# Layer 0 of a four-layer convolution kernel: columns evaluated at points as well as rows, and the weights of layers 1 and 2 kept in memory

## The chip, the cores and the metric

The kernel runs on one core of a Trainium2 chip. A core has five engines that run their own instruction streams in order: TensorE (PE in the profile) multiplies matrices into PSUM, VectorE (DVE), ScalarE (ACT) and GpSimd (POOL) work on elements, and SyncE (SP) issues most of the transfers. Transfers issued by SP and by ACT run on the same 16 DMA engines. The metric is the device time of one execution, in microseconds. The kernel before took 4069.13 us in the median of three runs (4066.38 to 4071.3).

## The reference, cut to what matters

The input is a batch of four images of 256 channels and 48 by 48 pixels. Four layers follow each other, each added to its input after a group normalisation. Only the first three concern us.

```
# layer 0: a 7x7 convolution, dilation 2, padding 6, 256 -> 128 channels
k = relu(conv(gn(x), w1, dilation=2, padding=6) + b1)
attn = softmax(relu(bn(conv1x1(k, w2) + b2)))          # 49 weights for each pixel
out  = sum over the 49 taps p of  shift(gn(x), p) * attn[p]
x = x + out
# layer 1: 3x3 convolution, sign of gn(x), sign of the weights
x = x + conv(sign(gn(x)), sign(wl1), padding=1)
# layer 2: 3x3 convolution with ternary weights and a scale for each output channel
x = x + conv(gn(x), alpha * ternary(wl2), padding=1)
# layer 3: windowed linear attention, unchanged here
```

## The kernel before, in words

**Layer 0.** A dilation of 2 splits an image into four phases (even and odd rows, even and odd columns), each a plain 24 by 24 image under a 7x7 convolution. The kernel computes the convolution by rows in the manner of Winograd and Toom-Cook: four output rows at a time, `MT = 4`, from seven evaluation points `POINTS = (0.0, None, 0.5, 1.0, -1.0, 2.0, -2.0)`, where `None` stands for infinity. For each point, VectorE combines input rows (`seen_at`, line 471 does the arithmetic), TensorE convolves the combined rows with the combined kernel rows (`conv0`, line 515), and VectorE adds the result, with a scale, into four output rows (lines 529 and 533). The seven kernel rows are handled as two parts (rows 0 to 3, rows 4 to 6), so every point but infinity has two parts. Along columns the convolution is direct: seven taps. One `conv0` call thus makes 2 parts x 2 halves of the image x 2 channel tiles x 7 taps = 56 matrix products of 288 output columns, and 28 at infinity.

**Weights of layer 0.** `transform_weights` (line 289 for arithmetic, line 283 for the stores) computes the combined kernel rows at the five points that are neither 0 nor infinity and stores them in DRAM through the SP queue. `load_wt` (line 256) loads one part for each use into one of three buffers, `wtp`. The points 0 and infinity need no combination: their weights are loaded straight from the input.

**After the convolution.** `activate0` (line 540) makes `k1`. `attention` (lines 555 to 571) makes the 49 weights for a block of five phase rows and stores them as a band matrix in DRAM; its work tile `e` has two buffers. `apply0` (lines 616 to 637) loads the bands, transposes them and multiplies.

**Layers 1 and 2.** `prepare_layer1` and `prepare_layer2` compute the signs and the ternary weights once, with scales, and keep them in SBUF as `wl1_sb` and `wl2_sb`. `conv3x3` (line 650) uses them for every image. Layer 2 runs as two half images.

**Order.** The main loop goes over images. Within image b, the seven `conv0` calls are interleaved with the rest of image b-1: attention after the first, `apply0` after the second and third, layer 1 after the fourth, the two halves of layer 2 after the fifth and sixth. So the convolution of one image fills TensorE while the other image waits for something. For image 0, where there is no image before, `prepare_layer1` and `prepare_layer2` take those places. The row combinations of the next image's points 0 and infinity are made inside the last call but one. A scheduler then reorders instructions by its own estimates of time and fixes an order for each engine and queue; the tile pools add waits for free buffers. Layer 3 (line 126 for all its operations) is written in a fixed order and runs after all of this, from about 1640 us on.

The lines of the main loop that set the interleaving:

```
ahead = {1: (0.5,), 2: (1.0, -1.0), 4: (2.0, -2.0)}
for f, p in enumerate(POINTS):
    conv0(f, vs.pop(p), rows)
    if f in ahead:
        vs.update(seen_at(pads[b], ahead[f]))
    if f < len(rest):
        rest[f]()
```

Of the kernel before, what the change touches and what calls it, by code (L numbers as in the profile page):

```python
# [10 lines left out]
F32 = mybir.dt.float32  # L11
BF16 = mybir.dt.bfloat16
# [7 lines left out]
P = 128  # L20
# [18 lines left out]
MT = 4  # L39
# [5 lines left out]
NTH = NT // 2  # L45
# [84 lines left out]
def conv_preact_kernel(  # L130
# [35 lines left out]

    wt_d = {
        (f, part): dram.tile([C, K0, P], F32, tag=f"wt{f}_{part}", name=f"wt{f}_{part}")
        for f, p in enumerate(POINTS)
        for part in range(2)  # L170
        if p
    }
    x3_d = [dram.tile([C, H, W], F32, tag=f"x3_{b}", name=f"x3_d{b}") for b in range(B)]
# [3 lines left out]
    def rsqrt(r, t, n):  # L177

        s = small.tile([P, n], F32, tag=f"rsq_s{n}", name="rsq_s")
        u = small.tile([P, n], F32, tag=f"rsq_u{n}", name="rsq_u")  # L180
        nc.scalar.activation(s, t, AF.Sqrt)  # L181
        nc.vector.reciprocal(r, s)
        nc.vector.tensor_mul(u, t, r)
        nc.vector.tensor_mul(u, u, r)
        nc.vector.tensor_scalar(u, u, -0.5, 1.5, ALU.mult, ALU.add)
        nc.vector.tensor_mul(r, r, u)
# [37 lines left out]
    with (  # L224
# [3 lines left out]
        tc.tile_pool(name="vp", bufs=3) as vp,  # L228
        tc.tile_pool(name="wtp", bufs=3) as wtp,
        tc.tile_pool(name="op0", bufs=1) as op0,  # L230
        tc.tile_pool(name="ps_cv", bufs=3, space=PSUM) as ps_cv,
# [12 lines left out]
        def rows_at(a):  # L244

            return w1[:, a * K0 : (a + 1) * K0, :].rearrange("(ct p) k o -> p ct k o", p=P)

        def load_wt(f, part):
            wt = wtp.tile([P, NCT, K0, P], F32, tag="wt", name="wt")
            p = POINTS[f]  # L250
            if p:
                src = wt_d[f, part].rearrange("(ct p) k o -> p ct k o", p=P)
            else:
                src = rows_at((MT - 1 if p is None else 0) + MT * part)
            for ct in range(NCT):
                nc.sync.dma_start(out=wt[:, ct], in_=src[:, ct])
            return wt

        def transform_weights():

            at = {p: f for f, p in enumerate(POINTS)}
            n = 0
            with tc.tile_pool(name="wst", bufs=2) as wst:
                for ct in range(NCT):
                    for k0, k1 in ((0, 4), (4, K0)):
# [16 lines left out]
                        def put(p, part, t):  # L282
                            nc.sync.dma_start(
                                out=wt_d[at[p], part][ct * P : (ct + 1) * P, k0:k1, :],
                                in_=t.rearrange("p (k o) -> p k o", o=P),
                            )
# [13 lines left out]
                        for p in (1.0, 2.0):  # L300
                            even, odd = new("we", 2), new("wo", 2)
                            stt(even, g[2], p * p, g[0])
                            stt(odd, g[3], p * p, g[1])
                            for s in (p, -p):
                                t = new("wr", 4)
                                stt(t, odd, s, even)
                                put(s, 0, t)
                            stt(even, g[6], p * p, g[4])
                            for s in (p, -p):
                                t = new("wr", 4)  # L310
                                stt(t, g[5], s, even)
                                put(s, 1, t)
# [36 lines left out]
        wl1_sb = wts.tile([P, NCT, T1, C], BF16, name="wl1_sb")  # L349
        wl2_sb = wts.tile([P, NCT, T1, C], F32R, name="wl2_sb")  # L350
        alpha = wts.tile([P, NCT], F32, name="alpha")

        def prepare_layer1():
            stage = padp.tile([P, NCT, T1, C], F32, tag="pad", name="wl1_stage")
            nc.sync.dma_start(out=stage, in_=wl1.rearrange("(ct p) t o -> p ct t o", p=P))
            nc.scalar.activation(wl1_sb, stage, AF.Sign)

        def prepare_layer2():
# [34 lines left out]
            for i, (ct, g) in enumerate(groups):  # L393
# [7 lines left out]
                nc.vector.tensor_sub(wl2_sb[:, ct, 3 * g : 3 * g + 3], u, v)  # L401
# [98 lines left out]

        def conv0(f, v, rows):

            p = POINTS[f]
            parts = range(1 if p is None else 2)
            pss = [
                ps_cv.tile([P, NPH, NTH, HP], F32, tag="cv", name="cv0") for half in range(2)
            ]
            vt = v.rearrange("p c (f t) w -> p c f t w", t=NTP)
            for part in parts:
                wt = load_wt(f, part)  # L510
                for half in range(2):
                    t0 = NTH * half + part
                    for ct in range(NCT):
                        for k in range(K0):
                            nc.tensor.matmul(  # L515
                                pss[half],
                                wt[:, ct, k, :],
                                vt[:, ct, :, t0 : t0 + NTH, k : k + HP],
                                start=((part, ct, k) == (0, 0, 0)),
                                stop=((part, ct, k) == (parts[-1], NCT - 1, K0 - 1)),  # L520
                            )
            for half in range(2):
                src = pss[half].rearrange("p f t w -> p (f t w)")
                for j in range(MT):
                    if scales[f][j] == 0.0:
                        continue
                    dst = rows[:, half, j, :]
                    if any(scales[i][j] != 0.0 for i in range(f)):
                        nc.vector.scalar_tensor_tensor(  # L529
                            dst, src, scales[f][j], dst, ALU.mult, ALU.add  # L530
                        )
                    else:
                        nc.vector.tensor_scalar_mul(dst, src, scales[f][j])

        def activate0(rows):

            k1 = op0.tile([P, NPH, HP * HP], F32, tag="k1", name="k1")
            for half in range(2):
                for j in range(MT):
                    nc.scalar.activation(  # L540
                        k1.rearrange("p f (h t j w) -> p h j f t w", h=2, t=NTH, j=MT)[:, half, j],
                        rows[:, half, j, :].rearrange("p (f t w) -> p f t w", f=NPH, t=NTH),
                        AF.Relu,
                        bias=b1_sb,
                    )
            return k1
# [92 lines left out]
        def conv3x3(parts, w_sb, evacuate, first, rbs):  # L639


            for mo in range(NCT):
                for rb in rbs:
                    ps = ps_cv.tile([P, RB, W], F32, tag="cv", name="cv3")
                    n = 0
                    for ct in range(NCT):
                        for t in range(T1):
                            r0, c0 = rb * RB + t // 3 - first, t % 3
                            for pad in parts:
                                nc.tensor.matmul(  # L650
                                    ps,
                                    w_sb[:, ct, t, mo * P : (mo + 1) * P],
# [5 lines left out]
                    evacuate(ps, mo, rb)  # L658

        def layer1(xt, b):  # L660
# [15 lines left out]
            conv3x3([pad], wl1_sb, evacuate, 0, range(NRB))  # L676

        def layer2(xt, b):
# [14 lines left out]
            def half_image(half):  # L693
# [12 lines left out]
                for ct in range(NCT):  # L706
# [20 lines left out]
                    wl2_sb,  # L727
# [28 lines left out]
        with (  # L756
# [4 lines left out]
            for b in range(B + 1):  # L761
# [33 lines left out]
                rows = op0.tile([P, 2, MT, NPH * NTH * HP], F32, tag="rows0", name="rows0")  # L795
# [829 lines left out]
```

## Time and profile before

| what | value |
|---|---|
| median of the runs | 4069.13 us |
| profiled execution, its own time | 4058.38 us |
| its span (first to last instruction) | 4056.6 us |
| granted TensorE clock over the span, mean | 0.955 of full speed |
| TensorE busy | 3580.7 us (88%) |
| VectorE busy | 2179.4 us (54%) |
| ScalarE busy | 950.8 us (23%) |
| GpSimd busy | 1446.2 us (36%) |
| start to the end of image 0's convolution | about 257 us |
| one turn of the loop over images (from the first `conv0` of an image to that of the next) | 372 us (632 to 1004 to 1376) |

The page gives busy times over the span, and then the span in 40 equal slices of 101 us. Layers 0 to 2 take slices 1 to 16. The trace can be asked for single stretches: a timeline gives start, duration, engine, line, operation and tiles, the count of merged instructions, and in brackets how long the engine sat idle before and who released it. One matrix product in float32 leaves two records, so that 364 products for each image are 728 records.

### The profile page before, as it was taken

How to read it: one execution, taken by the hardware profiler on the slowest of the kernel's cores; microseconds unless marked ns; L12 is line 12 of the kernel's file. 1: busy time of each engine (PE TensorE's matmuls, PEld its weight loads, DVE VectorE, ACT ScalarE, POOL GpSimd, SP SyncE). 2: the span in 40 equal slices, each digit the busy share in tenths (PEclk: the TensorE clock that was granted, in tenths of full speed). 3: DMA queues.
4: the chain of work that ended last, by engine and by line, in shares of the span. 5: the costliest groups of instructions: out<-in, count | busy, mean ns of one | idle time of the engine just before them, and what ended most of it. 6: DMA issues, size and time to landing. Idle time of an engine off the chain costs nothing. (4 is left out here: it accounts for less than half of the span.)

```text
span 4056.6 us, 70470 instructions
## 1 busy us (share of the span) xinstructions
PE 3580.7 (88%) x27940; PEld 2141.2 (53%) x27940; DVE 2179.4 (54%) x4704; ACT 950.8 (23%) x1863; POOL 1446.2 (36%) x2097
## 2 busy tenths in 40 slices
PE   5999998999899788678888888889998999988898
PEld 4777696778768668333334343344444444444443
DVE  7633325324332222466776666676666766556655
ACT  0101100100010110344422233332334423233321
POOL 0000000010001001244777557765645766444432
PEclk9999999999899778899999999999999999999999
DMA  7334015102510402333345434444422444210211
GB/s 280 129 63 73 28 65 64 56 19 83 71 40 19 39 23 74 100 108 129 126 145 150 116 100 135 139 145 118 130 74 95 134 124 124 68 40 29 60 56 55
DMA packets 364763, 367.85 MB, mean 91 GB/s; under 512 B 187123, under 2 KB 327443, under 8 KB 362003
## 3 DMA queue, kind: packets, MB, share of 16 engines
q1 hardware_dynamic: 358771, 353.84, 31.3%
q10 hardware_dynamic: 5520, 8.00, 0.6%
q8 instruction: 222, 3.64, 0.4%
q0 software_dynamic: 144, 1.52, 0.2%
q14 instruction: 106, 0.87, 0.1%
HBM read 249.47 MB, written 115.30 MB: 90 GB/s over the span
## 5 line engine op out<-in xcount | busy, mean ns | idle before, releaser
L126 DVE TENSOR_TENSOR sm<-s,masks 128x112 f32<-128x112 f32 (+10 forms) x2592 | 1135.5, 493 | 800.6 <-PE s L126 349.5
L126 POOL TENSOR_TENSOR sm<-sm,masks 128x432 f32<-128x432 f32 (+14 forms) x1152 | 853.2, 754 | 984.2 <-ACT sm L126 713.0
L126 PE MATMUL s<-qs,ks 32*128 32x320 f32 (+3 forms) x5760 | 825.9, 502 | 202.4 <-DVE sm L126 143.2
L126 ACT COPY sm<-s 128x528 f32<-128x528 f32 (+2 forms) x1152 | 594.1, 534 | 1512.9 <-PE s L126 1220.9
L126 PE MATMUL acc<-sm,vs 128*32 128x384 f32 (+18 forms) x13440 | 882.4, 386 | 13.8 <-POOL sm L126 13.7
L515 PE MATMUL cv<-v,wt 128*128 128x288 f32 x2912 | 763.2, 417 | 29.1 <-DVE v L471 21.0
L126 PEld LDWEIGHTS s<-qs,ks 32*128 32x128 f32 x5760 | 369.6, 187 | 609.2 <-DVE sm L126 216.6
L515 PEld LDWEIGHTS cv<-v,wt 128*128 128x128 f32 x2912 | 546.9, 191 | 194.6 <-issue 19.2
L126 PEld LDWEIGHTS acc<-sm,vs 128*32 128x32 f32 x13440 | 355.6, 111 | 549.0 <-issue 348.1
L650 PE MATMUL cv<-pad,wl_sb 128*128 128x384 f32 (+1 forms) x2592 | 472.1, 344 | 17.3 <-ACT pad L721 12.1
L650 PEld LDWEIGHTS cv<-pad,wl_sb 128*128 128x128 f32 x1728 | 319.5, 192 | 18.3 <-issue 12.3
L459 POOL MEMSET v<- 128x192 f32 x28 | 8.3, 297 | 786.2 <-issue 421.3
L529 DVE SCALAR_TENSOR_TENSOR rows<-cv,rows 128x288 f32<-128x288 f32 x144 | 57.1, 451 | 284.4 <-PE cv L515 284.4
L126 POOL TENSOR_TENSOR pt<-pt 128x144 f32<-128x144 f32 x336 | 183.4, 546 | 23.1 <-DVE pt L126 1.0
L126 POOL TENSOR_TENSOR nhi<-nhi,nq 128x384 f32<-128x384 f32 x144 | 149.7, 1066 | 0.0
L683 DVE SCALAR_TENSOR_TENSOR x<-cv,alpha,x 128x384 f32<-128x384 f32 x48 | 29.7, 618 | 222.1 <-PE cv L650 222.1
L181 ACT ACTIVATE rsq_s<-gn_v 128x2 f32<-128x2 f32 x16 | 3.3, 203 | 556.7 <-DVE gn_v L208 556.6
L126 PE MATMUL out_ps<-o,wout_sb 128*128 128x384 f32 x288 | 123.2, 510 | 9.9 <-DVE o L126 5.9
L126 PE MATMUL proj_ps<-wv_sb,xn 128*128 128x256 f32 x288 | 87.5, 434 | 42.7 <-ACT vt L126 21.8
L627 PEld LDWEIGHTS ap<-seen,xT 120*128 120x128 f32 (+2 forms) x832 | 115.4, 221 | 13.7 <-ACT seen L620 11.8
L627 PE MATMUL ap<-seen,xT 120*128 120x120 f32 (+3 forms) x832 | 119.4, 306 | 1.9 <-ACT seen L620 1.8
L650 PEld LDWEIGHTS <-wl_sb 128*128 128x128 bf16 x864 | 84.9, 99 | 63.6 <-issue 4.8
(157 smaller groups left out, 2549.1 us busy)
## 6 DMA issues: line engine op xcount, KB each, us to landing
wt<-wt SPq DMA_DIRECT2D x80, 448.0 KB
kb_d<-pt SPq DMA_DIRECT2D x48, 576.0 KB
rc<-r_d SPq DMA_DIRECT2D x192, 144.0 KB
nhi<-kb_d SPq DMA_DIRECT2D x120, 192.0 KB
nlo<-kb_d SPq DMA_DIRECT2D x88, 192.0 KB
o_d<-stage SPq DMA_DIRECT2D x24, 576.0 KB
o<-o_d SPq DMA_DIRECT2D x24, 576.0 KB
xr<-x_d SPq DMA_DIRECT2D x33, 384.0 KB
```

The costliest lines, as they stand in the source:

```text
L126: return lambda *args, **kwargs: self.tc.keep_in_program_order(op(*args, **kwargs))
L181: nc.scalar.activation(s, t, AF.Sqrt)
L459: nc.gpsimd.memset(v[:, :, :, 0:PADP], 0.0)
L515: nc.tensor.matmul(pss[half], wt[:, ct, k, :], vt[:, ct, :, t0 : t0 + NTH, k : k + HP], start=((part, ct, k) == (0, 0, 0)), stop=((part, c ...
L529: nc.vector.scalar_tensor_tensor(dst, src, scales[f][j], dst, ALU.mult, ALU.add)
L627: nc.tensor.matmul(pf[:, f, a:e], xTs[k + i][:n, f, mo * P : (mo + 1) * P], seen[:n, 1 + i, a:e], start=(i == 0), stop=(i == near[-1]),)
L650: nc.tensor.matmul(ps, w_sb[:, ct, t, mo * P : (mo + 1) * P], pad[:, ct, r0 : r0 + RB, c0 : c0 + W], start=(n == 0), stop=(n == len(parts) ...
L683: nc.vector.scalar_tensor_tensor(xs, ps, alpha[:, mo : mo + 1], xs, ALU.mult, ALU.add)
```

## The change

Columns are now treated like rows: two output columns at a time (`MX = 2`), seven taps split as 2+2+3, and four column points (1, -1, 0 and infinity). `columns_at` makes, for each row point, four tensors of column combinations from `v` on VectorE. `conv0` then makes, for each column point, products with three combined taps (one at infinity) over a whole image, so 288 output columns as before, and combines four PSUM results into `y`, which then goes into the rows. The combined weights have four column variants for each row point, also at the row points 0 and infinity. They are made by `put_columns`, with additions on GpSimd and stores on the ACT queue. `load_wt` loads one column point at a time.

To make room, the weights of layers 1 and 2 no longer stay in SBUF: `prepare_layer1` and `prepare_layer2` write them to DRAM, and `load_wl1` and `load_wl2` load them again for every use into the same buffers as layer 0's weights, `wtp`, now four. `vp` goes from three buffers to two, the temporaries `we` and `wo` from two to one.

The core of the diff:

```diff
-        tc.tile_pool(name="vp", bufs=3) as vp,
-        tc.tile_pool(name="wtp", bufs=3) as wtp,
+        tc.tile_pool(name="vp", bufs=2) as vp,
+        tc.tile_pool(name="wtp", bufs=4) as wtp,
+        tc.tile_pool(name="yp", bufs=2) as yp,
...
+        def load_wt(f, g):
+            src = wt_d[f, g]
+            n = src.shape[1] * src.shape[2]
+            wt = new_wt()[:, 0 : NCT * n].rearrange("p (ct a) o -> p ct a o", ct=NCT)
+            nc.sync.dma_start(
+                out=wt, in_=src.rearrange("(ct p) a k o -> p ct (a k) o", p=P)
+            )
...
+        def put_columns(f, part, c0, c1, t, ks, new):
+            def put(g, k0, k1, v):
+                for ct in range(c0, c1):
+                    nc.scalar.dma_start(
+                        out=wt_d[f, g][ct * P : (ct + 1) * P, part, k0:k1, :], in_=v[:, ct - c0]
+                    )
+            n = c1 - c0
+            if ks[0] == 0:
+                pairs = t[:, :, 0:4, :].rearrange("p c (k i) o -> p c k i o", i=2)
+                g0, g1 = pairs[:, :, :, 0, :], pairs[:, :, :, 1, :]
+                for g in (1, -1):
+                    u = new("wu", [P, n, 2, P])
+                    for c in range(n):
+                        (nc.gpsimd.tensor_add if g > 0 else nc.gpsimd.tensor_sub)(
+                            u[:, c], g0[:, c], g1[:, c]
+                        )
+                    put(g, 0, 2, u)
+                put(0, 0, 2, g0)
+            if ks[1] == K0:
+                g0, g1, g2 = (t[:, :, 4 - ks[0] + i, :] for i in range(3))
+                e = new("wx", [P, n, P])
+                nc.gpsimd.tensor_add(e, g0, g2)
+                for g in (1, -1):
+                    u = new("wu", [P, n, P])
+                    (nc.gpsimd.tensor_add if g > 0 else nc.gpsimd.tensor_sub)(u, e, g1)
+                    put(g, 2, 3, u.unsqueeze(2))
+                put(0, 2, 3, g0.unsqueeze(2))
+                put(None, 0, 1, g2.unsqueeze(2))
...
+                for i, (p, part, a) in enumerate(((0.0, 0, 0), (0.0, 1, MT), (None, 0, MT - 1))):
+                    raw = op0.tile([P, NCT, K0, P], F32, tag=("k1", "rows0")[i % 2], name="w1_row")
+                    nc.scalar.dma_start(out=raw, in_=w1[:, a * K0 : (a + 1) * K0, :]...)
+                    put_columns(at[p], part, 0, NCT, raw, (0, K0), new_x)
...
+            for mo in range(NCT):
+                signs = new_wt().bitcast(BF16)...
+                nc.scalar.activation(signs, stage[:, :, :, mo * P : (mo + 1) * P], AF.Sign)
+                nc.sync.dma_start(out=wl1_d[mo], in_=signs)
...
+                ternary = new_wt()[:, 0 : 3 * NCT]
+                nc.vector.tensor_sub(ternary.rearrange("p t m o -> p t (m o)"), u, v)
+                for mo in range(NCT):
+                    nc.sync.dma_start(
+                        out=wl2_d[mo, ct, :, 3 * g : 3 * g + 3, :], in_=ternary[:, :, mo, :]
+                    )
...
+        def columns_at(v):
+            n = NPH * NTP - 1
+            vx = {}
+            for g in XPOINTS:
+                t = vp.tile([P, NCT, NPH * NTP, NXP], F32, tag="vx", name="vx", bufs=8)
+                dst = t[:, :, 0:n, :]
+                i, j = {1: (1, 2), -1: (2, 1), 0: (0, 2), None: (1, 3)}[g]
+                u, w = (v[:, :, 0:n, k : k + MX * (NXP - 1) + 1 : MX] for k in (i, j))
+                (nc.vector.tensor_add if g == 1 else nc.vector.tensor_sub)(dst, u, w)
...
+            for g in XPOINTS:
+                wt = load_wt(f, g)
+                ps = ps_cv.tile([P, NPH, NT, NX], F32, tag="cv", name="cv0")
+                todo = [(part, i, k, ct) for part in parts
+                        for i, k in enumerate(XPARTS[g]) for ct in range(NCT)]
+                for n, (part, i, k, ct) in enumerate(todo):
+                    nc.tensor.matmul(ps, wt[:, ct, part, i, :],
+                                     vx[g][:, ct, :, part : part + NT, k : k + NX], ...)
+                if g == 1:
+                    for j in range(MX):
+                        nc.scalar.mul(y[:, :, j], ps, 0.5)
+                elif g == -1:
+                    for j, sign in enumerate((0.5, -0.5)):
+                        nc.vector.scalar_tensor_tensor(y[:, :, j], ps, sign, y[:, :, j], ...)
+                elif g == 0:
+                    nc.vector.tensor_add(y[:, :, 0], ps, y[:, :, 0])
+                else:
+                    nc.vector.tensor_sub(y[:, :, 1], y[:, :, 1], ps)
...
+        def load_wl2(mo):
+            w_sb = []
+            for ct in range(NCT):
+                wt = new_wt()[:, 0:T1]
+                nc.sync.dma_start(out=wt, in_=wl2_d[mo, ct])
+                w_sb.append(wt.bitcast(F32R))
+            return w_sb
```

## The prediction

> **What bounds the kernel now.** I read the page's slices first, then the costliest groups, then TensorE's timeline through layers 0 to 2, then its waits there.
>
> The slices (40, 101 us each):
>
> ```profile
> PE   5999998999899788678888888889998999988898
> DVE  7633325324332222466776666676666766556655
> ...
> PEclk9999999999899778899999999999999999999999
> ```
>
> Layers 0 to 2 are slices 1 to 16: TensorE is full, VectorE two to three tenths busy. The change touches nothing after them, so layer 3's stretch (1640 to 4057 us) is taken as it is. The group it rests on, and its consumer:
>
> ```profile
> L515 PE MATMUL cv<-v,wt 128*128 128x288 f32 x2912 | 763.2, 417 | 29.1 <-DVE v L471 21.0
> L529 DVE SCALAR_TENSOR_TENSOR rows<-cv,rows 128x288 f32<-128x288 f32 x144 | 57.1, 451 | 284.4 <-PE cv L515 284.4
> ```
>
> The layer-0 products take 763.2 us, with 29.1 us idle before them in all; VectorE waits for them, not they for VectorE. TensorE's timeline (start, duration, count; idle before in brackets):
>
> ```profile
> 36.21 7.59 PE L515 MATMUL cv<-v,wt 128*128 128x288 f32 x24 [8.13 <-DMA wt<-in_w_dram]
> ...
> 90.22 29.68 PE L515 MATMUL cv<-v,wt 128*128 128x288 f32 x112 [9.95 <-DVE v L471]
> 119.74 1.46 PE L380 MATMUL abs_ps<-wl_tmp,ones 128*128 128x256 f32 x6
> ...
> 140.35 0.83 PE L409 MATMUL sum_ps<-ones,wl_tmp 128*128 128x1 f32 x6
> ...
> 305.42 1.81 PE L555 MATMUL lg<-w_sb,k 128*120 128x49 f32 x8 [6.35 <-DVE e L560]
> ...
> 527.32 27.90 PE L515 MATMUL cv<-v,wt 128*128 128x288 f32 x112
> ...
> 632.05 26.18 PE L515 MATMUL cv<-v,wt 128*128 128x288 f32 x98 [3.87 <-DVE v L471]
> ...
> 679.69 1.80 PE L555 MATMUL lg<-w_sb,k 128*120 128x49 f32 x8 [7.04 <-DVE e L560]
> ...
> 697.74 0.63 PE L616 MATMUL tra<-ident,rows 120*120 120x120 f32 x2 [5.73 <-DMA rows<-band_d]
> ```
>
> In image 0 the small products of layer 2's preparation (119.7 to 198 us) sit between convolution products; its convolution ends at 257. From image 1 on a turn takes 372.0 us, 344 to 350 of them TensorE work. What TensorE waits for between 250 and 1660 us (total, times, longest):
>
> ```profile
> PE lg L555 <- DVE e L560: 39.2, 9, 13.5
> PE tra L616 <- DMA rows<-band_d: 26.1, 9, 10.5
> ```
>
> So the loop is TensorE's, with small holes in attention that convolution products fill until they run out.
>
> **What the Trainium skill says.** "TensorE: Matmul & The Clock Gate", Part 1: after about 3.4 us of idling TensorE runs at half clock until about 3.4 us of work. The trace agrees: the logits after 6.35 us of idling took 1.81 us instead of 0.94. "DMA: Bandwidth & Descriptors", Anatomy of one DMA: a transfer has about 2 us of fixed cost, mostly the receipt of the write. Here the load that depends on a weight store ending its issue at 60.7 was issued at 63.25, 2.5 us later. "Trainium Kernel Development and Optimization", Key Constraints: queues of SP, ACT and POOL share 16 DMA engines, and several issuers save only issue time. No row of before shows ACT issuing in such a mass. "GPSIMD Engine Reference", 3.1: an elementwise addition is 1.96 times as slow there as on VectorE; the trace has 1.07 us against 0.56 for 384 elements.
>
> **Part 1: products removed, images 1 to 3.** Before 6 x 56 + 28 = 364 products an image; after, 40 at each of six points (3+3+3+1 taps, two parts, two channel tiles) and 20 at infinity, 260. That is 104 products or 208 records fewer. A warm stretch gives 27.90/112 = 0.249 us a record, the whole group 763.2/2912 = 0.262, cold stretches included. I take the second: 54.5 us an image, **-163.5** for three. All of it is on the bound. Runs of 12 columns in place of 24 I price at nothing, since both make 288 columns a product; bounds 0 and +0.05 us a record (0.30).
>
> **Part 2: image 0, which gains nothing.** Its start becomes weight-bound. All column variants are now made: about 61 GpSimd additions of 256 elements at 0.67 us and 60 of 128 at about 0.5 are 71 us; VectorE, before it reaches layer 2's preparation, has 88 row combinations (0.53), 27 row points (0.845), 16 column combinations (1.05) and small work, 98 us from 46 on, so not before 143. The ACT queue has some 182 weight stores, 7 raw loads and a few activations ahead of layer 1's signs. With three `wu` buffers a result costs 0.67 (add) + 0.45 (issue) + 2.5 (store lands) = 3.7 us for a buffer, 1.2 us each; 80 of them are 98 us from 50 on, and the three raw loads behind each other on the same queue add some 17: **165 us** for the last store, 0.82 us an ACT entry. Below: 143, where VectorE and GpSimd set it. Above: 1.3 us an entry, 244.
>
> Queued behind it: the signs of layer 1 (ACT, 4.0 us), then SP's stores of those signs, behind which stand loads of point 0.5's later column weights. TensorE so resumes about 175. The rest of that point is 14 us (189). Then six groups of absolute sums (2.55 pitch, 15.3: 204), threshold and copies 2.7, and six groups of sums at 9.0 (pitch 9.8 before, less the 0.8 of convolution between), 54: 261. In the changed instruction order all sums stand ahead of the convolution of point 1.0 except its first column pairs, so TensorE mostly idles where it used to convolve. A cold clock adds 8 (269), and four points at 80 records x 0.249 = 19.9 end at **349** against 257: **+92**.
>
> **Part 3: the turns, +50.** A point's convolution is now 20 us, not 28, and two points surround attention. Turn 0 to 1: column combinations and padding of the next image have 4 us of convolution above them instead of 20, +5; attention's next block waits for its band store (about 11 us to land) with 30 us of filler, not 42, +5. Turns 1 to 2 and 2 to 3: in the changed order VectorE's padding and row points of the next image stand behind attention's first `e`, which waits for the logits, for `k1` and so for all of the last `conv0`. From its end: y 0.8, rows 3.6 (four of 576 elements at 0.75 and the normalisation), `k1` 2.8, logits 1.8, `e` 1.2, padding 3.25, row points 13.5, first columns 1.0: 28 us idle, before 1.37 + 3.87. That is +23; attention begins earlier and saves 6 of its 14 us of holes, +17 a turn, **34**. Cold restarts at 3 each: 6. Sum 10 + 34 + 6.
>
> Costed at nothing, with their cover: VectorE's additions, per point four columns x 1.07, four y operations x 0.45, four rows x 0.75 less eight x 0.45, +5.5 us, 36 an image; 132 becomes 168 of about 320. Two ACT multiplications a point (about 0.5). Both lie under 20 us of products; without that cover 5.5 and 1 a point. Weight loads: 2.6 MB a point and 5.9 MB for layers 1 and 2, against a DMA share of 0.22 to 0.26 in the loop; four buffers of at least 5 us each are issued 14 us ahead. If those loads came late, each point would lose what it lacks of 20 us. Layer 2's halves: a chain of 13 us under 20 (under 28 before). After image 3 nothing moves.
>
> **Sum.** 4056.6 + 92 + 50 - 163.5 = 4035 for the span; the median of the runs lies 12.5 above this span (4069.1, the profiled execution 4058.4). **4048**.
>
> **Rivals.**
> *A, the stores are quick and the turns hardly stall.* Last store at 143 (-22), turns +10 (-40): 3986. For it: GpSimd idle until slice 9; against: `e` before the padding in the order.
> *B, slower: the ACT store queue.* One mechanism at the start: every entry of about 190 issues more slowly than 0.82 us, because each waits for its addition on GpSimd, whose buffer waits for an earlier store. It decides from 0.95 us an entry (last store at 186: 21.5 us more, all the margin). At 1.3 us, 244, it gives 4127. For it: stores of 512-byte to 1 KB rows, with SP's loads on the same engines; against: DMA share three tenths there before.
> *C, the turns eat half of the gain* (weights for layers 1, 2 and 0 arrive late through one SP queue): 81 us lost, about 4130. Against: share 0.25.
> *D, the change does not do what it says:* a product over 12-column runs costs more. At 0.30 us a record 0.05 x 2080 = 104: 4150. Against: other shapes in the trace run at their column count.
>
> **How the numbers follow.** Forecast case, 4010 to 4061: 0.40. A: 0.12. Within 0.2% (4061 to 4077), what a measurement of this kernel can just tell from no change: 0.13. B: 0.23. C and D: 0.12. So faster 0.52, same 0.13, slower 0.35. The time is the first case's, 4048; its own range is 4010 to 4061. For 8 in 10, A reaches down to 3995 and B up to 4135; that leaves out half of A, D and the slowest of B.
>
> **What the profile after would show.** 2080 records of layer-0 products at 0.25 to 0.26 us (part 1, D). The last weight store on ACT near 165 and TensorE free from idling near 175 (part 2; 143 is A, beyond 186 B). TensorE mostly idle during the sums, image 0's convolution over near 349. Idle of 26 to 28 us before the first products of images 2 and 3, ended by VectorE's columns (A: below 10). A turn of 372 - 54.5 + 17 + 3 = about 338. Products released by weight loads in the loop would be C. Layer 3 unchanged at 2417. The prediction is wrong if the pace of ACT's entries leaves 0.7 to 0.95, if the scheduler's order leaves TensorE other work during the sums, or if the hole at a turn is not one chain.

## The result

The changed kernel takes 4117.26 us in the median of four runs (4107.39 to 4120.82). The kernel before, run beside it, takes 4070.22 (4066.38 to 4078.06). The ratio is 1.0109, interval 1.0086 to 1.0133: slower by about 1.1%, or 47 us, where 21 us less were forecast. The time lies inside the wide range given (3995 to 4135), outside that of the forecast case (4010 to 4061), and on the other side of no change. The profiled executions have spans of 4118.6 and 4056.6 us, a difference of 62: that of after is the slowest of its four runs (4120.8), that of before (4058.4) quicker than any run listed, so the sums below, made between profiles, are some 15 us too large in all.

Where the 62 us are, with the ends of convolutions taken from TensorE's timelines by counting records:

| stretch, us | before | after | difference | forecast |
|---|---|---|---|---|
| start to the end of image 0's convolution | 256.9 | 386.8 | +129.9 | +92 |
| from there to the end of image 3's convolution | 1113.2 | 1040.2 | -73.0 | -113.5 |
| the rest | 2686.5 | 2691.6 | +5.1 | 0 |

**The slices of after**, 40 of 103 us, in the order of those shown of before:

```profile
PE   3169889699788969578888898889989989988998
DVE  7645532752653222356777657676666775656655
POOL 4500000001000001244678747775646675444332
PEclk9569899799889979799989999999999999999999
```

TensorE is busy three tenths and one tenth in the first two slices, where it was full before, and its clock falls there and in each turn (a turn is one pass of the loop over images). GpSimd, idle at the start before, has the column weights to make.

**The costliest groups of after**: the layer-0 products, and the new column combinations that feed them.

```profile
L612 PE MATMUL cv<-vx,wt 128*128 128x288 f32 x2080 | 557.4, 425 | 119.5 <-DVE vx L592 65.2
L592 DVE TENSOR_TENSOR vx<-v 128x868 f32<-128x868 f32 x112 | 120.8, 1091 | 35.6 <-PE cv L612 35.6
```

The change does what it says: 2080 records for 2912, 205.8 us of work less, or 51.5 an image. But the idle before these products went from 29.1 to 119.5 us, and VectorE now releases much of it.

**TensorE's timeline of after**, through image 0, and at the turn from image 1 to image 2 (start, duration, count, idle before):

```profile
63.88 22.68 PE L612 MATMUL cv<-vx,wt 128*128 128x288 f32 x80 [32.19 <-DVE vx L592]
89.50 10.66 PE L612 MATMUL cv<-vx,wt 128*128 128x288 f32 x36 [2.94 <-issue]
146.58 2.29 PE L612 MATMUL cv<-vx,wt 128*128 128x288 f32 x4 [46.42 <-ACT y L622]
197.46 1.53 PE L698 MATMUL trx<-ident,pad 128*120 128x128 f32 x6 [48.59 <-ACT xT L703]
198.78 21.72 PE L612 MATMUL cv<-vx,wt 128*128 128x288 f32 x80
...
240.95 1.44 PE L490 MATMUL sum_ps<-ones,wl_tmp 128*128 128x1 f32 x6 [6.43 <-DVE wl_tmp L485]
...
252.48 1.44 PE L490 MATMUL sum_ps<-ones,wl_tmp 128*128 128x1 f32 x6 [5.02 <-DVE wl_tmp L485]
...
370.95 15.87 PE L612 MATMUL cv<-vx,wt 128*128 128x288 f32 x64
...
576.92 19.67 PE L612 MATMUL cv<-vx,wt 128*128 128x288 f32 x80
...
753.62 22.56 PE L612 MATMUL cv<-vx,wt 128*128 128x288 f32 x80 [16.49 <-DVE vx L592]
```

Two row points are done by 149 us, with a hole of 46 us in them; then nothing until 197; from 241 to 301 only the small sums of layer 2's preparation, with no convolution between them, each group at 1.44 us instead of 0.72. Once TensorE is warm (at full clock), a point takes 19.67 us for its 80 records.

What ended the two holes is in **ACT's timeline of after**, the queue's issues and its own work in one order:

```profile
146.09 0.43 ACT L622 ACTIVATE y<-cv 128x288 f32<-128x288 f32 x1 [4.59 <-DMA wt<-wr]
...
192.29 0.45 ACTq L276 DMA_DIRECT2D wt_None<-wr  x1
192.79 4.13 ACT L430 ACTIVATE wt<-wl_stage 128x2304 bf16<-128x2304 f32 x2 [46.27 <-DMA wt<-wu]
196.84 1.05 ACT L703 COPY xT<-trx 120x512 f32<-120x512 f32 x2
```

The last weight store is issued at 192.3; layer 1's signs and the copies that TensorE's transposes wait for stand behind it. Why no convolution runs beside the sums is in **SP's timeline of after**:

```profile
284.15 0.89 SPq L480 DMA_DIRECT2D wl_d<-wt  x2
285.14 0.46 SPq L265 DMA_DIRECT2D wt<-wt  x1
```

The first column weights of point 1.0 are loaded (L265) at 285.1, after the fifth of the six stores of ternary weights (L480).

### The profile page after: what moved, and what is told of

It is laid out like the page before. It is cut to its first block, busy times and chain, and to the rows that moved or that the text cites. A ratio compares the mean times of both kernels' runs of the same rounds, so it can differ in the third digit from the quotient of the medians.

```text
span 4118.6 us, 69754 instructions
## 1 busy us (share of the span) xinstructions
PE 3411.3 (83%) x27108; PEld 2021.9 (49%) x27108; DVE 2354.4 (57%) x4840; ACT 968.8 (24%) x1904; POOL 1552.0 (38%) x2218
## 5 line engine op out<-in xcount | busy, mean ns | idle before, releaser
L612 PE MATMUL cv<-vx,wt 128*128 128x288 f32 x2080 | 557.4, 425 | 119.5 <-DVE vx L592 65.2
L612 PEld LDWEIGHTS cv<-vx,wt 128*128 128x128 f32 x2080 | 406.0, 199 | 235.2 <-DVE vx L592 65.9
L759 PE MATMUL cv<-pad,wt 128*128 128x384 f32 (+1 forms) x2592 | 479.0, 348 | 18.7 <-ACT pad L844 6.1
L759 PEld LDWEIGHTS cv<-pad,wt 128*128 128x128 f32 x1728 | 324.5, 195 | 17.5 <-issue 12.5
L806 DVE SCALAR_TENSOR_TENSOR x<-cv,alpha,x 128x384 f32<-128x384 f32 x48 | 29.7, 618 | 220.9 <-PE cv L759 220.9
L592 DVE TENSOR_TENSOR vx<-v 128x868 f32<-128x868 f32 x112 | 120.8, 1091 | 35.6 <-PE cv L612 35.6
L759 PEld LDWEIGHTS <-wt 128*128 128x128 bf16 x864 | 85.9, 100 | 66.8 <-issue 10.2
L133 PE MATMUL out_ps<-stage,wout_sb 128*128 128x384 f32 x288 | 117.9, 491 | 0.6 <-DVE stage L133 0.6
L735 PE MATMUL ap<-seen,xT 75*128 75x75 f32 (+3 forms) x832 | 114.9, 299 | 2.3 <-ACT seen L728 1.9
```

The costliest lines, as they stand in the source:

```text
L133: return lambda *args, **kwargs: self.tc.keep_in_program_order(op(*args, **kwargs))
L592: (nc.vector.tensor_add if g == 1 else nc.vector.tensor_sub)(dst, u, w)
L612: nc.tensor.matmul(ps, wt[:, ct, part, i, :], vx[g][:, ct, :, part : part + NT, k : k + NX], start=(n == 0), stop=(n == len(todo) - 1),)
L735: nc.tensor.matmul(pf[:, f, a:e], xTs[k + i][:n, f, mo * P : (mo + 1) * P], seen[:n, 1 + i, a:e], start=(i == 0), stop=(i == near[-1]),)
L759: nc.tensor.matmul(ps, w_sb[ct][:, t, :], pad[:, ct, r0 : r0 + RB, c0 : c0 + W], start=(n == 0), stop=(n == len(parts) * NCT * T1 - 1),)
L806: nc.vector.scalar_tensor_tensor(xs, ps, alpha[:, mo : mo + 1], xs, ALU.mult, ALU.add)
```

## The experiments

The theory: image 0 is held by two separate things, the ACT queue with its stores until 197 us, and after that layer 2's sums, which no longer run beside convolution; and each turn is held by a hole that 20 us of convolution cover less well than 28 us did. The rivals stand in each expectation. The runs were made on other chips than the first comparison; the kernel before took 4055 to 4058 us beside them, so ratios are compared.

**e1: layer 2's ternary weights kept out of the ring of weight buffers.** In the changed order they are given a buffer of `wtp` six times (the four buffers are handed out in a ring) between the weights of point 0.5 and those of point 1.0.

```diff
-            tmp = padp.tile([P, 4, 3, C], F32, tag="pad", name="wl2_tmp")
+            tmp = padp.tile([P, 8, 3, C], F32, tag="pad", name="wl2_tmp")
...
-                ternary = new_wt()[:, 0 : 3 * NCT]
-                ternary = ternary.rearrange("p (t m) o -> p t m o", t=3)
-                nc.vector.tensor_sub(ternary.rearrange("p t m o -> p t (m o)"), u, v)
+                nc.vector.tensor_sub(tmp[:, 4 + i % 4], u, v)
+                ternary = tmp[:, 4 + i % 4].rearrange("p t (m o) -> p t m o", m=NCT)
```

> The ternary weights of layer 2 no longer pass through the four weight buffers; they stay in unused room of the staging tile. Theory R (the ring of weight buffers is why TensorE stands between 220 and 306 us: point 1.0's column weights wait for buffers that hold ternary weights still to be made): products of the last four points (80 us) run among the sums again, the convolution of image 0 ends near 325 instead of 387, the median falls by about 60 to 4057. Rival V (the two buffers of row points, or VectorE itself, hold point 1.0): the end stays within 10 us of 387, the time within 10 of 4117.

Measured: 4029.28 us, ratio 0.9928 (0.9905 to 0.9951). Image 0 ends at 325.4. TensorE's timeline of e1, at the sums:

```profile
242.54 0.83 PE L489 MATMUL sum_ps<-ones,wl_tmp 128*128 128x1 f32 x6
243.23 1.22 PE L611 MATMUL cv<-vx,wt 128*128 128x288 f32 x4
244.28 0.72 PE L489 MATMUL sum_ps<-ones,wl_tmp 128*128 128x1 f32 x6
...
309.98 15.37 PE L611 MATMUL cv<-vx,wt 128*128 128x288 f32 x62
```

The convolution runs between the sums again, TensorE stays at full clock (0.72 us for a group), and 61 us are back. Theory R holds. With these few lines changed, the kernel is 0.7% faster than the one before: the sign of the result hung on the ring.

**e4: the other way round, the kernel before with only the weights of layers 1 and 2 streamed.** `prepare_layer1`, `prepare_layer2` and `conv3x3` as in the change, layer 0 as before.

```diff
-        wl1_sb = wts.tile([P, NCT, T1, C], BF16, name="wl1_sb")
-        wl2_sb = wts.tile([P, NCT, T1, C], F32R, name="wl2_sb")
...
-                nc.vector.tensor_sub(wl2_sb[:, ct, 3 * g : 3 * g + 3], u, v)
+                ternary = new_wt()[:, 0 : 3 * NCT]
...
+                    nc.sync.dma_start(
+                        out=wl2_d[mo, ct, :, 3 * g : 3 * g + 3, :], in_=ternary[:, :, mo, :]
+                    )
```

> The kernel before with one part of the change alone: the weights of layers 1 and 2 written to memory once and loaded for every use into the weight buffers (four of 7 KB). Theory R: the sums of image 0 run without convolution products between them again, since point 1.0's weights wait for the same buffers: image 0 ends about 60 us later (257 to 317), the turns stay at 372, the time about 4130. Rival: the loads and stores hide and the order holds: 4070; or the loads delay each turn by 5 to 10: 4085 to 4100 with image 0 at 257.

Measured: 4137.29 us, ratio 1.0196 (1.0179 to 1.0214). Image 0 ends at 334.3 instead of 256.9, +77, and the three turns take 1118.3 us instead of 1113.2, +5. TensorE's timeline of e4:

```profile
103.34 1.96 PE L603 MATMUL trx<-ident,pad 128*120 128x128 f32 x8 [20.17 <-ACT xT L608]
105.91 30.43 PE L528 MATMUL cv<-v,wt 128*128 128x288 f32 x112 [0.61 <-DMA wt<-wt]
...
202.92 1.44 PE L422 MATMUL sum_ps<-ones,wl_tmp 128*128 128x1 f32 x6 [5.02 <-DVE wl_tmp L417]
...
222.47 83.67 PE L528 MATMUL cv<-v,wt 128*128 128x288 f32 x328
```

The same picture without any column weights: the sums alone, then the convolution in one piece. Of the 17 us beyond the 60 expected for image 0, 16 are a later start of point 0.5 (105.9 for 90.2): TensorE waits for `xT`, behind the signs on ACT, and that point's weights are loaded only from 101.5 on, behind the stores of the signs on SP, so that the one wait hides another. Reloading the weights so costs about 5 us in the turns, and making them by way of memory and the shared buffers 77 of the 82 us. The rest of the change takes the ratio from 1.0196 to 1.0109, a gain of about 35 us.

**e3: no weights made for layer 0.** `load_wt` takes raw kernel rows and `transform_weights` is not called.

```diff
-                out=wt, in_=src.rearrange("(ct p) a k o -> p ct (a k) o", p=P)
+                out=wt, in_=w1[:, 0:n, :].rearrange("(ct p) n o -> p ct n o", p=P)
...
-        transform_weights()
```

> Left out: every combination of layer-0 weights, row and column, with its loads and stores; each product uses raw kernel rows of the same size instead. It measures what making the weights costs in all. If the stores hold image 0 (my theory): TensorE starts near 45 and runs three points in one piece (50 us), the sums follow at the pitch of 11.5, image 0 ends near 265 instead of 387, the time is about 3995. If rather VectorE's row points and columns, or the raw loads' absence, matter little: the end stays above 330 and the time above 4060.

Measured: 3969.07 us, ratio 0.9779 (0.9753 to 0.9805); image 0 ends at 259.8, and the sums still run alone. Making the weights, with all that belongs to it (raw loads, both engines' combinations, stores), costs 127 us of image 0 in the changed order. These 127 and the 61 of e1 are not the same microseconds: the one ends at 197, the other begins at 241.

**e6: the stores without GpSimd's additions.** The stores take uncombined columns.

```diff
-                    u = new("wu", [P, n, 2, P])
-                    for c in range(n):
-                        (nc.gpsimd.tensor_add if g > 0 else nc.gpsimd.tensor_sub)(
-                            u[:, c], g0[:, c], g1[:, c]
-                        )
-                    put(g, 0, 2, u)
+                    put(g, 0, 2, g1)
```

> Left out: GpSimd's additions and subtractions of weight columns, and with them the three result buffers; the stores take uncombined columns in their place, as many and as large as before. If the pace of the stores (0.98 us an entry) is that of the additions and of the buffers they wait for: the last store goes from 192 to about 148, where VectorE's row combinations end, image 0 ends near 345, the ratio falls by 0.010 to 1.000. If it is the issue itself or the landing of stores beside the raw loads: last store beyond 180, ratio within 0.003 of 1.011.

Measured: 4067.43 us, ratio 1.0012 (0.9998 to 1.0027); image 0 ends at 352.5. ACT's timeline of e6:

```profile
154.75 0.45 ACTq L276 DMA_DIRECT2D wt_None<-wr  x1
155.24 0.73 ACT L613 ACTIVATE y<-cv 128x288 f32<-128x288 f32 x2 [29.95 <-DVE gn_st L206]
```

The last store comes 37.5 us earlier, the end of image 0 34 us: the pace was that of the additions with their buffers, and not of the issue. Additions and buffers went together here; e11 comes back to the buffers. VectorE, whose code is the same, also became faster. The groups up to 200 us, of after and then of e6:

```profile
L592 DVE TENSOR_TENSOR vx<-v 128x868 f32<-128x868 f32 x16 | 21.0, 1315 | 0.0
```

```profile
L583 DVE TENSOR_TENSOR vx<-v 128x868 f32<-128x868 f32 x20 | 20.9, 1057 | 4.8 <-PE cv L603 4.8
```

A column combination took 1.32 us beside GpSimd's additions and 1.06 without them, and the row combinations of weights 0.73 to 0.91 us and 0.62.

**e2: the raw loads on SP's queue.** `nc.scalar.dma_start` becomes `nc.sync.dma_start` at lines 327 and 338.

> Only the seven loads of raw layer-0 weights go from the ACT queue to the SP queue. Theory Q (column stores land late because they stand behind a raw load on the same queue; the waits of GpSimd for a free result buffer of 8 to 11 us are those): these waits fall to about 2.5 us each, the last store goes from 192 to about 165, the time falls by about 25 to 4092. Rival P (the pace is set by the additions, three result buffers and the issue itself): last store within 5 us of 192, time within 10 of 4117. It is slower than 4117 if the loads, waiting for their buffers, block SP.

Measured: 4095.01 us, ratio 1.0094 (1.0074 to 1.0114); the last store at 186.4. Rival P holds, with the last store a microsecond beyond its bound: GpSimd waited less for its buffers, but 30.0 us for raw rows instead of 12.3.

**e5: the stores on SP's queue.** The same edit at line 276.

> Only the stores of the column weights go from the ACT queue to the SP queue. Theory H (what holds TensorE until 197 us is that ACT's own work, the two multiplications for y, layer 1's signs and the copies of xT, stands in order behind some 180 stores): the waits of TensorE for y (46 us) and xT (49 us) vanish, point 0.5 starts when its weights are there (about 155 at the earliest), image 0 ends near 350 instead of 387, the time falls by 35 in the ratio to before, to about 1.002. Rival S (the weights are late wherever they are stored from, or SP's loads now stand behind the stores): the end stays within 10 us of 387 or comes later, the ratio stays at 1.009 or above.

Measured: 4095.13 us, ratio 1.0097 (1.0079 to 1.0114); image 0 ends at 389.4, though the last store came at 178.5. ACT was free of stores, and TensorE's waits changed their name. TensorE's waits in e5 up to 385 us (total, times, longest):

```profile
PE cv L612 <- DMA wt<-wt: 60.6, 3, 48.4
PE cv L612 <- DMA wt<-wt_None: 35.1, 1, 35.1
PE sum_ps L490 <- DVE wl_tmp L485: 31.5, 6, 6.4
PE trx L698 <- ACT xT L703: 27.8, 1, 27.8
```

The products now wait for loads that stand behind the stores on SP: rival S. Which queue it is is not the point; whichever holds the stores holds up what stands behind them.

**e10: e1, with TensorE's early needs taken off ACT.** In image 0 the multiplications for `y` and the copies of `xT` go to VectorE, and both preparations come one call later.

```diff
-                    rest = [lambda: None, prepare_layer1, prepare_layer2]
+                    rest = [lambda: None, lambda: None, prepare_layer1, prepare_layer2]
...
-                        nc.scalar.mul(y[:, :, j], ps, 0.5)
+                            nc.vector.tensor_scalar_mul(y[:, :, j], ps, 0.5)
...
-                nc.scalar.copy(xT[:q, 2 * h : 2 * h + 2, :], tr)
+                    nc.vector.tensor_copy(xT[:q, 2 * h : 2 * h + 2, :], tr)
```

> As e1, and in image 0 the two multiplications for y and the copies of xT run on VectorE, and layer 1's signs and layer 2's preparation come one call later, so that nothing TensorE waits for before point 1.0 stands behind ACT's stores. Theory H2 (e5 only moved the block to SP; the weights of point 0.5 themselves are there near 160): point 0.5 runs near 160 to 180 instead of 200 to 221, the sums start near 210 and image 0 ends near 290 instead of 326; ratio about 0.984. Rival S (the last weights set it): the end within 10 us of 326, ratio within 0.003 of 0.993.

Measured: 4021.57 us, ratio 0.9916 (0.9886 to 0.9945), not to be told from e1. Point 0.5 did start 33 us earlier than in e1, at 166.8, and the convolution ended at 305.0 instead of 325.4. TensorE's timeline of e10 there:

```profile
303.79 1.22 PE L611 MATMUL cv<-vx,wt 128*128 128x288 f32 x4
304.84 1.04 PE L700 MATMUL trx<-ident,pad 128*120 128x128 f32 x8
326.37 0.64 PE L665 MATMUL lg<-w_sb,k 128*120 128x49 f32 x2 [20.50 <-ACT k L650]
```

The 20 us came back as one wait. VectorE turns to the padding and the row points of image 1 only when the sums are done (306 to 323 us), and the rows that `k1` needs stand behind them; in e1 that work lay under the last point. e11 adds four `e` buffers and five result buffers for GpSimd:

> e9 and e10 together, and five result buffers for GpSimd instead of three. If the three act where I think: last store near 178 instead of 193, image 0 over near 275, ratio near 0.975, about 3960 where before takes 4060. If E and H2 both fall: within 0.004 of e1's 0.993.

Measured: 4030.95 us, ratio 0.9944 (0.9923 to 0.9965), with image 0's activation at 322.3 against 323.5 in e10. The last store came at 186.4, in e10 at 186.8: with five buffers GpSimd waited only 11 us for stores to land (56 in after), but 23 us for raw rows and 23 for VectorE's combined rows. So three buffers alone did not set the pace.

**e7: the turn, without the statistics of images 1 to 3.** `make_pad0` uses those of image 0.

```diff
-            m, r = gn_stats(xt, ps_st)
+            if b == 0:
+                stats0.extend(gn_stats(xt, ps_st))
...
+            m, r = stats0
```

> Left out: the statistics of the input of images 1 to 3 (each is normalised with those of image 0), so 12 reductions of VectorE, 7.6 us, and the chain of small operations behind them, some 4 us, for each turn. Theory C (the idle of 16.5 us ahead of the first products of images 2 and 3 is one VectorE chain from the arrival of the next image: statistics, padding, row points, first column): the idle falls to about 5 us at each, the time by 20 to 30. My prediction's reading (the padding stands behind attention's first e, after the last product of the old image) leaves the idle at 14 to 17 and the time within 8.

Measured: 4063.13 us, ratio 1.0017 (1.0006 to 1.0028), 0.9% or some 37 us under the changed kernel. VectorE's timeline of after at image 2, from the arrival of the image to its first columns:

```profile
720.81 2.86 DVE L206 BATCH_NORM_STATS2 gn_st<-x 128x6 f32<-128x384 f32 x6 [0.58 <-DMA x<-in_x_dram]
...
734.87 0.36 DVE L668 TENSOR_TENSOR e<-lg,bn_inv 120x196 f32<-120x196 f32 x1 [1.24 <-PE lg L663]
...
735.85 3.24 DVE L517 TENSOR_SCALAR pad<-x,gn_m,gn_r 128x1152 f32<-128x1152 f32 x4
...
752.51 3.98 DVE L592 TENSOR_TENSOR vx<-v 128x868 f32<-128x868 f32 x4
```

and TensorE's and VectorE's of e7 at the same place:

```profile
687.43 16.84 PE L620 MATMUL cv<-vx,wt 128*128 128x288 f32 x68
716.50 18.72 PE L620 MATMUL cv<-vx,wt 128*128 128x288 f32 x70 [12.23 <-issue]
697.75 1.67 DVE L525 TENSOR_SCALAR pad<-x,kept,kept 128x1152 f32<-128x1152 f32 x2 [0.34 <-DMA x<-in_x_dram]
```

From the last product of one image to the first of the next, after has 26.5 us (727.1 to 753.6, of which 4.4 are logits and sums), e7 12.2. The idle did not fall to 5 as theory C had it, since the 16.5 shown was only part of the hole. Between profiles the three turns take 17 us less than those of e5 and 37 less than those of after.

e7 does not separate theory C from the reading of the prediction. In after, the padding (L517) does stand behind attention's first `e` (L668), as forecast; but the statistics of the new image, which begin at 720.8, when it has arrived, are finished hardly earlier, and without `e` the padding could have begun less than 2 us sooner (an estimate from the 1.24 us of waiting for the logits and the 1.0 us of three operations on `e`). In e7, free of the statistics, the order has the padding at 697.8, before the old image's last product, so that both chains are gone at once. What both have in common is the arrival: in after the load of the new image is issued at 714.0, some 6 us after the store of image 0, which lay in the same one of the two buffers (issued at 707.8), and the 33 us of VectorE's work behind it have 6 us of convolution left above them.

**e8, e9 and e12: the waits of attention.** e8 moves the band stores and loads to ACT's queue (`nc.sync` to `nc.scalar` at lines 682 and 718).

> Only the stores and loads of attention's band matrices go from the SP queue to the ACT queue. Theory W (on SP they stand behind weight loads that wait for a free buffer, which the change made more numerous): TensorE's waits for the band rows between 387 and 1431 us fall from about 44 to 20 us and those for e too, the time falls by 20 to 30. Rival L (the landing of a band store, 11 us, sets these waits): they stay, the time within 8 of 4117; it grows if ACT, waiting in order, delays the exponentials and copies.

Measured: 4108.13 us, ratio 1.0127 (1.0107 to 1.0147). The waits for band rows fell from 40.8 to 13.3 us between 326 and 1435 us, but 12.3 us of waits for copies on ACT came in their place, those for `e` grew from about 15 to 29.7, and image 3's attention, which has no convolution over it, took longer: 309 us from its activation to layer 3's first scores instead of 296.

e9 gives `e` four buffers, on top of e1 (`bufs=4` at line 664; the threshold tile moves into `tmp`).

> As e1, and attention's work tile e has four buffers instead of two (its room comes from the threshold tile of layer 2, moved into the staging tile). Theory E (in the stage of attention a block waits until the band store of the block two before has landed, some 11 us, which 20 us products no longer cover): TensorE's waits for e go from about 33 us in all turns to under 10, the ratio to before from 0.993 (e1) to about 0.987. Rival L: the wait only moves to the band rows, which need the same stores; the sum of the two waits falls by less than 10 us and the ratio stays within 0.003 of e1's.

Measured: 4028.59 us, ratio 0.9942 (0.9922 to 0.9961). TensorE's waits between 326 and 1435 us, which takes in most of image 3's attention, of e1 and then of e9:

```profile
PE tra L723 <- DMA rows<-band_d: 41.7, 9, 11.0
PE cv L611 <- DVE vx L591: 33.0, 2, 16.5
PE lg L662 <- DVE e L667: 27.5, 9, 11.8
```

```profile
PE tra L723 <- DMA rows<-band_d: 83.4, 7, 36.2
```

The wait for `e` is nearly gone (2.7 us) and that for the rows has doubled, 36 us of it in one piece in image 3: rival L. Both edits together:

> e9 with the band stores and loads on the ACT queue, as in e8. Each alone moved attention's waits from one tile to the other and saved nothing. Theory EW (two limits in series: two buffers of e, and the weight loads ahead of the bands on SP): with both gone TensorE's waits for e and for band rows in the turns together fall from about 54 us (e1) to under 20, the sum of the three turns from 1015 (e1) to below 990, the ratio to before to about 0.987. Rival L (the latency of store and load of a band is the limit whichever queue and however many buffers): waits of e, rows and the copies seen together stay above 45 us, ratio within 0.003 of e1's 0.993.

Measured: 4029.93 us, ratio 0.9934 (0.9912 to 0.9956). Between 326 and 1345 us the waits for `e`, rows and the copies `seen` make 37 us, against 41 us for the first two in e1; the three turns take 1006 us instead of 1015, but image 3's attention takes 294 instead of 288, and nothing is seen in the time. Neither expectation is met to the letter. The waits of attention only moved in all three runs; what would shorten them was not found.

## Why the prediction was wrong

**Part 1, the products: right, a little smaller.** 208 records an image went, as counted, at 0.246 us when warm (0.249 before), so runs of 12 columns cost nothing and rival D falls. The saving was 51.5 us an image and not 54.5, since the records that are left carry as much half clock as before: 154 instead of 163.5 for three.

**Part 2, image 0: the order of events held, and four terms were too small.** The step that failed first is the price of the weight stores. The last one came at 192.3, not 165: 0.98 us an entry and not 0.82, past the point (0.95) from which rival B was to decide. What was mis-sized is GpSimd's additions, priced at 71 us in all. In after they take 106.6, most of it here:

```profile
L287 POOL TENSOR_TENSOR wu<-wr 128x256 f32<-128x256 f32 x40 | 44.5, 1136 | 27.1 <-DMA wt<-wu 10.7 <-DMA wt_-1_79<-wu 8.8 <-DMA wt_-1_95<-wu 3.4
```

An addition of 256 elements was priced at 0.67 us and took 1.14 here; the column combinations on VectorE were priced at 1.05 and took 1.32. e6 shows that VectorE worked more slowly while GpSimd added; that GpSimd was slowed by VectorE in the same way is likely, and no run shows it alone. The rest of the 27 us, the waits for buffers, for raw rows and for VectorE, was not taken apart: e6, e2 and e11 show that neither the issue, nor the queue of the raw loads, nor the three buffers was the limit by itself.

What resumed at 199 was all of point 0.5, 21.6 us, not the 14 us left of it, because transposes stood ahead of it in TensorE's order and their copies behind the signs on ACT. The path named in the forecast, SP's stores of the signs, lay close behind: that point's loads were issued at 191.2 and from 197.4 on. The threshold took 6.4 us and not 2.7, as it had in before already (133.9 to 140.4 us), so that term was misread. And the sums took 65 us (241 to 306) and not 54, 11.5 a group and not 9.0: that figure came from a trace in which TensorE was warm, and the 0.8 us of convolution was taken off but not the half clock put on, at which the four parts of a group took 1.44 us each and not 0.72. The 8 us for a cold clock put down elsewhere did not come. Together 386.8 instead of 349.

That all sums would stand ahead of the convolution was foreseen, and read as a matter of the order. What was missed is why: the ring of four buffers. e4 and e1 show it from both sides, and that it is worth 61 us of the changed kernel, more than its whole loss.

**Part 3, the turns: the other step that failed.** The forecast was -113.5 and the profiles have -73.0. Of the 50 us of stalls forecast, 44 were idle time and 6 cold restarts. By the windows of both profiles, TensorE's idle in the turns rose by about 65 us, and its work fell by 138 us where 157.5 were forecast. TensorE's waits in the turns of after, from 392 to 1428 us (total, times, longest):

```profile
PE tra L724 <- DMA rows<-band_d: 40.8, 9, 14.9
PE cv L612 <- DVE vx L592: 33.0, 2, 16.5
PE gn_ps L219 <- DVE gn_v L217: 25.5, 8, 4.5
PE lg L663 <- DVE e L668: 14.9, 5, 7.4
```

In the turns of before (257 to 1370 us) the same four are 15.5, 10.5, 13.0 and 21.0 us. Put against the forecast, the rise of the idle time is:

| part, us in three turns | forecast | measured |
|---|---|---|
| holes between images, all waits in them | +51 | +37 |
| band rows | +5 | +25 |
| statistics of layers 1 and 2 | 0 | +8 |
| attention's `e` | -12 | -6 |
| other | 0 | +1 |

So the hole between images was not the miss. It was even over-priced; the chain named there stands in the trace, but a second one, the statistics of the new image, was not in the forecast and ends within 2 us of it. What failed is the wait for band rows, which was given 5 us, in one turn only. The statistics it did not have at all: in VectorE's order of after, work of the convolution stands among the small operations of layer 2's statistics,

```profile
597.12 2.76 DVE L638 SCALAR_TENSOR_TENSOR rows<-y,rows 128x576 f32<-128x576 f32 x4
...
599.87 1.06 DVE L592 TENSOR_TENSOR vx<-v 128x868 f32<-128x868 f32 x1
```

and TensorE waits 4.5 us there instead of 2.2, once a turn. As for the work, the products fell by 154 us, and what is left grew by 16 where 6 were forecast, since TensorE runs at a clock of 0.90 to 0.91 and not 0.95 to 0.97 (the first 80 records after a hole took 22.6 us instead of 19.7, the logits twice their time).

Part of the size is of this execution and its chip: with the same code for the turns, e1, e5 and e6 show waits of 28.6 to 30.3 us for band rows and turns of 1007 to 1015 us together instead of 1036, so some 20 to 30 us of the 40 missed are not seen everywhere.

**What was priced at nothing.** The two multiplications stayed hidden, and so did VectorE's additions, but for the statistics just shown. Reloading the weights cost about 5 us in e4's turns; in after no product in a turn waited for weights by the profile.

**The rivals.** The forecast of faster failed by B at the start (27 us of it), by the other terms of image 0, and by a loss in the turns like C's, though not by C's mechanism: no weights were seen to come late there. B's own reading, a buffer that waits for an earlier store, is only part of its pace (e11). A fell with the first holes.

## What to carry to other kernels

A temporary that borrows a buffer from a rotating pool takes its place in that pool's order: everything allocated later waits until the temporary is done, however unrelated; count the allocations between two uses, as one counts instructions. Work priced from a stretch in which TensorE was warm has to be priced again for a stretch in which it will be alone, and VectorE's work, priced alone, again for a stretch in which GpSimd will add beside it (1.06 us became 1.32 here). When a long stream of stores is given to an engine's queue, list what that engine computes behind it and who waits; moving the stream to another queue moves the list, and removing one hole shows the next one in line.

## What the runs showed that was not expected

Three edits that each removed or cut a visible wait of TensorE (46 and 49 us on ACT in e10, 27.5 us for `e` in e9, 27 of 41 us for band rows in e8) changed the time by nothing that could be measured; one that removed no wait listed for the products by name, the six buffers taken from a ring in e1, changed it by 1.8%. The trace names the last releaser of an instruction, not of the order in which it was put.
